# A gated delta-rule transformer block on one core: the keys' squared norms from one wide squaring and a sum along the rows, together with a later read of a scratch block, one more step in the key stage, an earlier half of the output squares, and other buffer counts

## Chip, cores, metric

The kernel runs on one core of a Trainium2 chip. The metric is device time in microseconds (us) of one execution. The kernel before took 2166.83 us, the median of 3 runs (2163.37 to 2167.89).

## What is computed

The reference is one adaptive-layernorm block over x of shape 8 x 256 x 256 (batch, tokens, channels). A small matrix product of a conditioning vector gives shifts, scales and gates. The first half is a gated delta-rule attention with 16 key heads of width 128 and 32 value heads (two for each key head):

```python
qkv_c = sum((xp[:, j:j + Tq, :] * conv_w[:, j] for j in range(KC)))      # causal convolution, 4 taps
q = _l2norm(qkv_c[..., :QD].reshape(Bq, Tq, NK, DK))
k = _l2norm(qkv_c[..., QD:2 * QD].reshape(Bq, Tq, NK, DK))
def step(S, inp):
    q_t, k_t, v_t, b_t, d_t = inp
    Sk = jnp.einsum('bhi,bhipj->bhpj', k_t, S)
    dv = b_t[..., None] * (v_t - Sk)
    S = S * d_t[:, :, None, :, None] + jnp.einsum('bhi,bhpj->bhipj', k_t, dv)
    return (S, jnp.einsum('bhi,bhipj->bhpj', q_t, S))
out = out * rms * norm_w                       # rms over each value head
y = (out * silu(z)) @ W_out.T
```

The second half is a gated feed-forward of inner width 1024 in which the two largest magnitudes of every four are kept. All arithmetic is in float32.

## The kernel before

**Tiling.** Two batch rows (512 tokens) are treated together as one pair; there are 4 pairs. Four key heads are one group, so there are 16 groups. The recurrence is rewritten in chunks of 128 tokens: for every chunk a triangular matrix built from k k^T and the decays is inverted, first in 32 x 32 blocks and then, by levels, up to 128 x 128.

**Stages of a head.** `stage_a` (L479) prepares a key head of the next group: projection `ps_k` (L432), convolution to `k_t` (ScalarE L418, three VectorE steps L420), squared norms (`norms2`, L441), the row `bk` (L507), the diagonal `diag` on GpSimd (L516), a scan `e` on VectorE (L551), the matrix `a_t` (L563), and four DMAs of its diagonal blocks to the scratch `scr` in DRAM (L572). Its `yield`s are the points at which other work is put in between. `stage_b` (L577) runs once a group: it loads the scratch of all four heads as `blk` (L584), makes the negated transpose `xb` of it on ScalarE (L586), solves the 32 x 32 blocks by 30 pairs of VectorE instructions (L592, L598), and stores two results (L602, L604). `levels` (L662) reads them back (L675, L678, L681) and merges the blocks on TensorE, beginning with `ps_w` (L691). `prepare` (L607) makes queries, values and gates of a head (`cv`, `gz`). `attend` (L752), once for each of the pair's two rows, makes the outputs `o`, their mean squares `ss` (L845), a reciprocal root on GpSimd, and `og` (L861). `shares` (L883) multiplies by the output weights. `feed_forward` (L160) and `fill` (L262) take tokens through a pool `feed_pool`; the last four feed-forward units run in the pool `tail`.

**The squared norms.** `norms2` transposes a 128 x 512 tile by TensorE into one PSUM bank and then, for each of its four 128 x 128 parts, runs a ScalarE squaring with an accumulator output (L451). It is called for the keys (`n2k`) by `stage_a` and for the queries (`n2q`) by `prepare`. The bank is one of three that `ps_in` has; the projections `ps_qv`, `ps_k`, the gates `ps_z` and the shares `ps_y` use the same three.

**What sets the order.** The loop over heads keeps a list of generators and takes one step of each in turn; after each turn it calls `along()` (L1073), which advances the background of the next group (`ahead`, L967: all `stage_a` steps at cost 3.0 each, all `stage_b` steps at cost 1.0 each) until its done cost reaches a share of `work` (L997), so that the background is due after three quarters of the group's 32 nominal turns. A scheduler then takes this order as priorities, assigns buffers, and lays down one fixed order of instructions for each engine. An instruction that waits holds up all that stands behind it on its engine or DMA queue.

The lines around `work` and its use:

```python
work = 3.0 * 4 * GH + Q
while done < work * rounds / (total * 3 / 4):
    step = next(background, None)
```

Of the kernel before, what the change touches and what calls it, by code (L numbers as in the profile page):

```python
# [11 lines left out]
F32 = mybir.dt.float32  # L12
AF = mybir.ActivationFunctionType
ALU = mybir.AluOpType
AX = mybir.AxisListType
# [3 lines left out]
P = 128  # L19
# [5 lines left out]
Q = 32  # L25
NQ = P // Q
GH = 4
# [21 lines left out]
def adaln_block(  # L49
# [18 lines left out]
    nc = tc.nc  # L68
    NT, C = x.shape
# [3 lines left out]
    NCH = T // P  # L73
# [9 lines left out]
    small = ctx.enter_context(tc.tile_pool(name="small", bufs=4))  # L83
# [76 lines left out]
    def feed_forward(pool, b, n, y_all, w_bufs=3):  # L160
# [3 lines left out]
        gate = pool.tile([P, C], F32, tag="gate", name="gate")  # L164
        nc.sync.dma_start(out=gate, in_=gate_dram[b, 0].partition_broadcast(P))
        yield
        yg = pool.tile([P, 1, C], F32, tag="tokens", name="yg")
        nc.vector.tensor_tensor(out=yg[:, 0, :], in0=y_all[:, b % 2 * NCH + n, :], in1=gate, op=ALU.mult)
        nc.vector.tensor_tensor(out=x1, in0=x1, in1=yg, op=ALU.add)
        gate = pool.tile([P, C], F32, tag="gate", name="gate")  # L170
        nc.sync.dma_start(out=gate, in_=gate_dram[b, 1].partition_broadcast(P))
        xn = pool.tile([P, 1, C], F32, tag="tokens", name="xn")
        normed(xn, x1)
        yield
        h2 = pool.tile([P, CC, P], F32, tag="h2", name="h2")
# [4 lines left out]
        for j in range(NG):  # L180
            hj = hid[:, j]
            for i in range(0, 4, 2):
                ps = bank(ps_inv, [P, 2, 2, P], "ps_ff")
                for a in range(2):
# [14 lines left out]
                    out=hj[:, i : i + 2], in0=hj[:, i : i + 2], in1=ps[:, 1], op=ALU.mult  # L199
# [10 lines left out]
            for lag, cmp in ((1, c1), (2, c2), (3, c3)):  # L210
                nc.vector.tensor_tensor(
                    out=cmp, in0=mag[:, : 4 - lag], in1=mag[:, lag:], op=ALU.is_ge
# [12 lines left out]
                out=d[:, 2:4], in0=d[:, 2:4], scalar=1.0, in1=c2, op0=ALU.add, op1=ALU.subtract  # L225
            )
            yield
            for i, m, least in ((0, 3, 1.5), (3, 1, -0.5)):
                nc.vector.scalar_tensor_tensor(
                    out=hj[:, i : i + m],  # L230
# [7 lines left out]
        ps = bank(ps_inv, [P, C], "ps_out")  # L238
        for j in range(NG):
            for i in range(0, 4, 2):  # L240
                w = pool.tile([P, 2, C], F32, tag="w_ff", name="w_dn", bufs=w_bufs)
                nc.sync.dma_start(out=w, in_=w_down[j, i // 2])
                for l in range(2):
# [4 lines left out]
                        start=(j + i + l == 0),  # L248
                        stop=(j == NG - 1 and i + l == 3),
                    )  # L250
        res = pool.tile([P, C], F32, tag="tokens", name="res")
        nc.vector.tensor_tensor(out=res, in0=gate, in1=ps, op=ALU.mult)
        nc.vector.tensor_tensor(out=res, in0=res, in1=x1[:, 0, :], op=ALU.add)
        nc.sync.dma_start(out=out_v[:, NCH * b + n, :], in_=res)
# [7 lines left out]
    def fill(pool, bp, h_bp, xs):  # L262
# [4 lines left out]
        for i in range(2):  # L267
            b = 2 * bp + i
            for n0 in range(0, NCH, NCH if xs else 1):
                n1 = NCH if xs else n0 + 1  # L270
                if xs:
                    x1, xn = xs[0][:, NCH * i : NCH * (i + 1)], xs[1][:, NCH * i : NCH * (i + 1)]
                else:
                    x1 = pool.tile([P, 1, C], F32, tag="x1", name="x0")
                    xn = pool.tile([P, 1, C], F32, tag="tokens", name="xn0")
                nc.sync.dma_start(out=x1, in_=x_v[:, NCH * b + n0 : NCH * b + n1, :])
                normed(xn, x1)
                yield
                done = modulated(xn, b, h_bp[:, :, i * T + n0 * P : i * T + n1 * P], 0)
                if bp == 0:  # L280
                    begun["tokens"] = done
                yield
        NT4 = 2 * NCH
        ps = bank(ps_mix, [P, NT4, 2, NV], "ps_ba")
        for n in range(NT4):
# [14 lines left out]
            out=a_pre,  # L300
            in0=ps[:, :, 1, :],
            in1=bias_bc[:, None, :].to_broadcast([P, NT4, NV]),
            op=ALU.add,
# [10 lines left out]
            out=y, in0=w, scalar=-1.0, in1=y, op0=ALU.add, op1=ALU.subtract  # L314
# [22 lines left out]
        ps = bank(ps_mix, [NV, NT4, P], "ps_dt")  # L337
# [14 lines left out]
        ps = bank(ps_mix, [P, 2, 2, NV], "ps_g")  # L352
# [13 lines left out]
    with ExitStack() as scope:  # L366
# [4 lines left out]
        mixp = scope.enter_context(tc.tile_pool(name="mixp", bufs=4))  # L371
# [69 lines left out]
        def norms2(src, name):  # L441

            n2 = small.tile([P, 2, NCH], F32, tag=name, name=name)
            ps = bank(ps_in if name == "n2k" else ps_in, [P, 2, NCH, P], f"ps_{name}")
            for i in range(2):
                for n in range(NCH):
                    nc.tensor.transpose(ps[:, i, n, :], src[:, i, n * P : (n + 1) * P], ident)
            for i in range(2):
                for n in range(NCH):
                    junk = mixp.tile([P, P], F32, tag="junk", name="junk", bufs=2)  # L450
                    nc.scalar.activation(  # L451
                        junk, ps[:, i, n, :], AF.Square, accum_out=n2[:, i, n : n + 1]
                    )
            return n2
# [24 lines left out]
        def stage_a(kh, bp, hp, wk, h_bp, scr):  # L479
# [16 lines left out]
            else:  # L496
# [11 lines left out]
                out=bk,  # L508
# [13 lines left out]
            with tc.issue_after(done.ins):  # L522
                nc.gpsimd.tensor_tensor(out=nk, in0=n2f, in1=halves[:, : 2 * NCH], op=ALU.pow)
            yield rec

            e = rec_pool.tile([P, 2, NS, PE1], F32, tag="e", name="e")
            rec["e"] = e
# [46 lines left out]
                )  # L574
            yield rec

        def stage_b(scr, scr_x, scr_y):  # L577

            blk = single.tile([P, Q, Q], F32, tag="blk", name="blk")
            nc.sync.dma_start(out=blk, in_=scr)  # L584
            xb = single.tile([P, Q, Q], F32, tag="xb", name="xb")
            nc.scalar.activation(xb, blk.rearrange("p a b -> p b a"), AF.Copy, scale=-1.0)  # L586
            nc.gpsimd.memset(xb.rearrange("p a b -> p (a b)")[:, :: Q + 1], 1.0)
            yield
            for j in range(1, Q - 1):
                m = Q - 1 - j  # L590
                tmp = single.tile([P, m, j], F32, tag="tmp", name="tmp", bufs=2)
                nc.vector.tensor_tensor(  # L592
                    out=tmp,
                    in0=blk[:, j, j + 1 :, None].to_broadcast([P, m, j]),
                    in1=xb[:, j, None, 0:j].to_broadcast([P, m, j]),
                    op=ALU.mult,
                )
                solved = nc.vector.tensor_tensor(  # L598
                    out=xb[:, j + 1 :, 0:j], in0=xb[:, j + 1 :, 0:j], in1=tmp, op=ALU.subtract
                )  # L600
                yield solved.ins
            nc.sync.dma_start(out=scr_x, in_=xb)  # L602
            nc.scalar.copy(blk, xb.rearrange("p a b -> p b a"))
            nc.sync.dma_start(out=scr_y, in_=blk)  # L604
            yield
# [146 lines left out]
        def attend(rec, i, cv, gz, eps_q, tt, og_t):  # L752
# [71 lines left out]
            for h in range(2):  # L824
                nc.tensor.matmul(ps_o[:, h, :], lhsT=aq[:, 0, h, :], rhs=u0[:, h, :], start=True, stop=True)  # L825
            nc.scalar.copy(o[:, 0], ps_o)
            yield

            ps_u = bank(ps_mix, [P, 2, P], "ps_u1")
# [8 lines left out]
            nc.vector.tensor_tensor(out=o[:, 1], in0=o[:, 1], in1=ps_o, op=ALU.add)  # L838


            ss = small.tile([P, NCH, 2], F32, tag="ss", name="ss")
            for n in range(NCH):
                for h in range(2):
                    junk = mixp.tile([P, P], F32, tag="junk", name="junk", bufs=2)
                    nc.scalar.activation(  # L845
                        junk, o[:, n, h, :], AF.Square, accum_out=ss[:, n, h : h + 1]
                    )
            nc.vector.scalar_tensor_tensor(  # L848
                out=ss,
                in0=ss,  # L850
# [143 lines left out]
            yield from fill(feed_pool, bp, h_t, None)  # L994
            nc.sync.dma_start(out=h_dram[bp], in_=h_t)

        work = 3.0 * 4 * GH + Q  # L997
        recs, scratch = [], []
        xs = [rec_pool.tile([P, 2 * NCH, C], F32, tag="a_t", name=f"xs{i}", bufs=5) for i in range(2)]
        sel = selectors()  # L1000
# [204 lines left out]
```

## Time and profile before

| what | value |
|---|---|
| median of 3 runs | 2166.83 us |
| the profiled execution's own time | 2163.81 us |
| its span in the profile | 2162.0 us |
| granted TensorE clock | 0.987 of full speed |
| chain that ended last, by engine | PE 64%, ACT 12%, DVE 11%, DMA 7%, issue 4% |
| DMA queue q1 | 163.34 MB, 28.2% of 16 engines' span |
| DMA issue blk<-scr, 16 times 512 KB | 3.6 us from issue to landing |
| DMA issue scr<-a_t, 256 times 32 KB | 2.6 us from issue to landing |

PE is TensorE's matmul, PEld its weight load, DVE VectorE, ACT ScalarE, POOL GpSimd, SP the engine that issues most DMAs. In a row of groups the columns are: line, engine, operation, output<-inputs with shapes and count; then busy us in all and mean ns of one; then the engine's idle time just before these instructions and what ended it. In a row of waits: the engine and line that waited, what it waited for, us in total, times, the longest in us. In a row of windows: the stretch in us, its length, busy us of each engine (with the number of instructions), granted clock, DMA share and GB/s. Ends of matmuls are modelled, and a float32 matmul shows as two records.

### The profile page before, as it was taken

The numbers are of one execution on the slowest core, as the hardware profiler recorded it, in microseconds if no ns is written. First come the engines' busy times: TensorE is split into PE (matmuls) and PEld (weight loads), VectorE is DVE, ScalarE is ACT, GpSimd is POOL, SyncE is SP. The second block draws the span as 40 slices with busy tenths as digits, with TensorE's granted clock in tenths as the row PEclk, the third lists the DMA queues.
The fourth block names the chain that finished last, engine by engine and source line by source line (L and its number), as shares of the span: only waits on it lengthen the run. The fifth ranks groups of instructions, "written<-read, shape, count | busy, mean of one in ns | idle before, by whom it ended". The sixth has DMA issues, their size and how long they took to land.

```text
span 2162.0 us, 46431 instructions
## 1 busy us (share of the span) xinstructions
PE 2061.9 (95%) x16684; PEld 1634.1 (76%) x16684; DVE 1663.1 (77%) x4039; ACT 1373.6 (64%) x4552; POOL 370.7 (17%) x375
## 2 busy tenths in 40 slices
PE   8889999999999999999999999999999989999998
PEld 5567777777777777778777787787878777787887
DVE  6688686877869578797878868788797868879457
ACT  3577676866656566666566656666676666666652
POOL 3120212112120111212121121211202012121010
PEclk9999999999999999999999999999999999999999
DMA  4242423333342443434434343443434344343336
GB/s 137 85 117 65 105 68 101 91 83 91 101 117 67 124 115 95 132 90 109 119 90 118 104 109 94 122 117 87 132 92 108 92 115 120 108 113 90 75 91 212
DMA packets 324517, 226.85 MB, mean 105 GB/s; under 512 B 254520, under 2 KB 266168, under 8 KB 324288
## 3 DMA queue, kind: packets, MB, share of 16 engines
q1 hardware_dynamic: 304416, 163.34, 28.2%
q10 hardware_dynamic: 19872, 60.54, 8.8%
q8 instruction: 133, 2.18, 0.4%
q14 instruction: 96, 0.79, 0.1%
HBM read 186.28 MB, written 29.12 MB: 100 GB/s over the span
## 4 chain that ended last, share of the span: by engine, by line
PE 64%; ACT 12%; DVE 11%; DMA 7%; issue 4%; SPq 1%; POOL 1%; ACTq 0%; DVEq 0%; POOLq 0%
PE ps_y L891 9%; PE ps_qv L432 8%; PE ps_z L634 8%; PE ps_ks L806 5%; PE ps_ff L190 3%; PE ps_k L432 3%; PE ps_o L825 2%; PE ps_u L831 2%; DVE cv L420 2%; PE ps_out L244 2%; DMA blk<-scr 2%; PE ps_kk L532 2%; DMA scr<-a_t 2%; PE ps_u L798 2%; DVE a_t L563 2%
## 5 line engine op out<-in xcount | busy, mean ns | idle before, releaser
L420 DVE SCALAR_TENSOR_TENSOR cv<-ps_qv,conv_sb,cv 128x510 f32<-128x510 f32 (+1 forms) x564 | 410.2, 737 | 43.5 <-ACT cv L418 39.4
L432 PE MATMUL ps_qv<-h_bp,wh 128*128 128x512 f32 x768 | 365.1, 601 | 12.0 <-ACT junk L451 8.4
L105 POOL TENSOR_TENSOR rs<-ss,minus_halves 128x4 f32<-128x4 f32 x128 | 135.2, 1058 | 1019.6 <-DVE ss L848 1018.6
L634 PE MATMUL ps_z<-wh,h_bp 128*128 128x256 f32 x1024 | 250.4, 390 | 9.5 <-ACT junk L451 6.6
L891 PE MATMUL ps_y<-wo,og_p 128*128 128x256 f32 x1024 | 236.8, 380 | 0.8 <-ACT og_p L878 0.8
L432 PEld LDWEIGHTS ps_qv<-h_bp,wh 128*128 128x128 f32 x768 | 133.3, 191 | 118.9 <-issue 99.3
L634 PEld LDWEIGHTS ps_z<-wh,h_bp 128*128 128x128 f32 x1024 | 189.1, 193 | 38.5 <-ACT junk L451 9.9
L891 PEld LDWEIGHTS ps_y<-wo,og_p 128*128 128x128 f32 x1024 | 187.4, 190 | 22.8 <-ACT og_p L878 1.1
L418 ACT ACTIVATE cv<-ps_qv,conv_sb 128x512 f32<-128x512 f32 x188 | 129.6, 690 | 117.6 <-PE ps_qv L432 117.0
L592 DVE TENSOR_TENSOR tmp<-blk,xb 128x30 f32<-128x30 f32 (+14 forms) x480 | 156.8, 327 | 57.8 <-ACT xb L586 48.7
L516 POOL TENSOR_TENSOR diag<-consts,bk 128x1032 f32<-128x1032 f32 x64 | 122.8, 1919 | 384.5 <-DVE bk L507 352.6
L845 ACT ACTIVATE junk<-o 128x128 f32<-128x128 f32 x512 | 153.3, 303 | 41.4 <-DVE o L838 35.0
L551 DVE TENSOR_TENSOR_SCAN e<-dbc,diag 128x1032 f32<-128x1032 f32 x60 | 137.9, 2298 | 39.3 <-POOL diag L516 36.3
L598 DVE TENSOR_TENSOR xb<-xb,tmp 128x30 f32<-128x30 f32 (+14 forms) x480 | 157.0, 327 | 9.5
L420 DVE SCALAR_TENSOR_TENSOR k_t<-ps_k,conv_sb,k_t 128x510 f32<-128x510 f32 (+1 forms) x189 | 139.7, 740 | 24.8 <-ACT k_t L418 22.9
L861 DVE SCALAR_TENSOR_TENSOR og<-o,rs,gz 128x128 f32<-128x128 f32 x512 | 145.9, 344 | 10.3 <-POOL rs L105 8.1
L772 ACT ACTIVATE vn<-ps_v,nk 128x256 f32<-128x256 f32 x256 | 106.2, 483 | 61.4 <-PE ps_v L767 61.2
L806 PE MATMUL ps_ks<-u,cross 128*128 128x128 f32 x1024 | 141.0, 280 | 0.9 <-ACT u L800 0.9
L806 PEld LDWEIGHTS ps_ks<-u,cross 128*128 128x128 f32 x1024 | 130.8, 194 | 9.5 <-issue 3.3
L190 PE MATMUL ps_ff<-h,w_ff 128*128 128x128 f32 x1024 | 130.0, 277 | 3.2 <-ACT h L149 2.2
L190 PEld LDWEIGHTS ps_ff<-h,w_ff 128*128 128x128 f32 x1024 | 122.5, 192 | 7.8 <-ACT h L149 3.2
L432 PE MATMUL ps_k<-h_bp,wk 128*128 128x512 f32 x256 | 124.9, 613 | 1.6 <-ACT junk L451 1.2
(177 smaller groups left out, 4274.8 us busy)
## 6 DMA issues: line engine op xcount, KB each, us to landing
wh<-in_w_heads ACTq DMA_DIRECT2D x64, 640.0 KB, 4.0
w_ff<-in_w_ff SPq DMA_DIRECT2D x128, 256.0 KB, 2.9
dbc<-d_dram SPq DMA_DIRECT2D x60, 516.0 KB, 4.3
wo<-in_w_heads ACTq DMA_DIRECT2D x32, 512.0 KB, 3.7
w_dn<-in_w_down SPq DMA_DIRECT2D x64, 256.0 KB, 3.8
wk<-in_w_keys SPq DMA_DIRECT2D x16, 512.0 KB, 4.5
scr<-a_t SPq DMA_DIRECT2D x256, 32.0 KB, 2.6
blk<-scr SPq DMA_DIRECT2D x16, 512.0 KB, 3.6
```

What stands on the lines that cost most here:

```text
L105: nc.gpsimd.tensor_tensor(out=out, in0=in_, in1=minus_halves[:, :n], op=ALU.pow)
L190: nc.tensor.matmul(ps[:, a, l, :], lhsT=w[:, k, l, :], rhs=h2[:, k, :], start=(k == 0), stop=(k == CC - 1),)
L420: nc.vector.scalar_tensor_tensor(out=dst[:, :, d:], in0=ps[:, :, : T - d], scalar=taps[:, KC - 1 - d : KC - d], in1=dst[:, :, d:], op0=ALU ...
L432: nc.tensor.matmul(ps.rearrange("p b t -> p (b t)"), lhsT=w[k], rhs=h_bp[:, k, :], start=(k == 0), stop=(k == CC - 1),)
L551: nc.vector.tensor_tensor_scan(e.rearrange("p i s t -> p (i s t)"), dbc.rearrange("p i f -> p (i f)"), diag.rearrange("p s t -> p (s t)"), ...
L592: nc.vector.tensor_tensor(out=tmp, in0=blk[:, j, j + 1 :, None].to_broadcast([P, m, j]), in1=xb[:, j, None, 0:j].to_broadcast([P, m, j]), ...
L598: solved = nc.vector.tensor_tensor(out=xb[:, j + 1 :, 0:j], in0=xb[:, j + 1 :, 0:j], in1=tmp, op=ALU.subtract)
L634: nc.tensor.matmul(ps[:, n, :], lhsT=h_bp[:, k, i * T + n * P : i * T + (n + 1) * P], rhs=wh[:, k * 640 + 384 : (k + 1) * 640], start=(k = ...
L806: nc.tensor.matmul(ps_ks[:, ct, h, :], lhsT=cross[:, h, ct, :], rhs=u0[:, h, :], start=True, stop=True)
L845: nc.scalar.activation(junk, o[:, n, h, :], AF.Square, accum_out=ss[:, n, h : h + 1])
L861: nc.vector.scalar_tensor_tensor(out=og[:, n, h, :], in0=o[:, n, h, :], scalar=rs[:, 2 * n + h : 2 * n + h + 1], in1=gz[:, i, n, h, :], op ...
L891: nc.tensor.matmul(ps_y[:, n, :], lhsT=og_p[:, j // 2, i, n, j % 2, :], rhs=wo[:, j // 2, j % 2, :], start=(j == 0), stop=(j == 3),)
```

## The change

Five edits:

1. **Key norms.** In `norms2`, for `n2k` alone, one ScalarE squaring of all 512 columns writes a tile `sq` (one buffer), and one VectorE `tensor_reduce` sums each of the four 128-column parts into `n2`. The queries keep the four squarings with accumulators.
2. **A later read of `blk`.** `stage_b` yields seven times (`LANDS`) between the issue of the load of `blk` and the ScalarE instruction that reads it; `work` grows from 80 to 99 to count these and the steps of edit 3.
3. **One more yield** in `stage_a` after the norms, except in the first group.
4. **Output squares.** In `attend` the two squarings of the first chunk's output are placed right after the copy that makes it, two yields earlier; those of the second chunk stay.
5. **Buffers.** The tag `tokens` has 2 buffers everywhere: before it had 1 in `feed_pool` and 4 in `tail`.

```diff
-        yg = pool.tile([P, 1, C], F32, tag="tokens", name="yg")
+        yg = pool.tile([P, 1, C], F32, tag="tokens", name="yg", bufs=2)
...
+            if name == "n2k":
+                sq = mixp.tile([P, 2, NCH, P], F32, tag="sq", name="sq", bufs=1)
+                nc.scalar.activation(sq, ps, AF.Square)
+                nc.vector.tensor_reduce(out=n2, in_=sq, axis=AX.X, op=ALU.add)
+                return n2
...
             yield rec
+            if not first:
+                yield rec
...
+        LANDS = 7
...
             nc.sync.dma_start(out=blk, in_=scr)
+            for _ in range(LANDS):
+                yield None
             xb = single.tile([P, Q, Q], F32, tag="xb", name="xb")
...
             nc.scalar.copy(o[:, 0], ps_o)
+            ss = small.tile([P, NCH, 2], F32, tag="ss", name="ss")
+
+            def squares(n):
+                for h in range(2):
+                    junk = mixp.tile([P, P], F32, tag="junk", name="junk", bufs=2)
+                    nc.scalar.activation(
+                        junk, o[:, n, h, :], AF.Square, accum_out=ss[:, n, h : h + 1]
+                    )
+
+            squares(0)
             yield
...
+            squares(1)
...
-        work = 3.0 * 4 * GH + Q
+        work = 3.0 * 5 * GH + Q + LANDS
```

The same `bufs=2` is given to `xn`, `xn0` and `res`.

More of the change, by code (lines that the diff above doesn't have):

```diff
@@ L171, in feed_forward @@
         nc.sync.dma_start(out=gate, in_=gate_dram[b, 1].partition_broadcast(P))
-        xn = pool.tile([P, 1, C], F32, tag="tokens", name="xn")
+        xn = pool.tile([P, 1, C], F32, tag="tokens", name="xn", bufs=2)
         normed(xn, x1)
@@ L250, in feed_forward @@
                     )
-        res = pool.tile([P, C], F32, tag="tokens", name="res")
+        res = pool.tile([P, C], F32, tag="tokens", name="res", bufs=2)
         nc.vector.tensor_tensor(out=res, in0=gate, in1=ps, op=ALU.mult)
@@ L274, in fill @@
                     x1 = pool.tile([P, 1, C], F32, tag="x1", name="x0")
-                    xn = pool.tile([P, 1, C], F32, tag="tokens", name="xn0")
+                    xn = pool.tile([P, 1, C], F32, tag="tokens", name="xn0", bufs=2)
                 nc.sync.dma_start(out=x1, in_=x_v[:, NCH * b + n0 : NCH * b + n1, :])
@@ L838, in attend @@
             nc.vector.tensor_tensor(out=o[:, 1], in0=o[:, 1], in1=ps_o, op=ALU.add)
[L841 to L847, printed above, removed]
+            squares(1)
             nc.vector.scalar_tensor_tensor(
```

## Prediction

> **What bounds the kernel now.** I read the busy shares first, then the waits, then the windows, then a timeline of one window.
>
> ```profile
> PE 2061.9 (95%) x16684; PEld 1634.1 (76%) x16684; DVE 1663.1 (77%) x4039; ACT 1373.6 (64%) x4552; POOL 370.7 (17%) x375
> ```
>
> TensorE is the bound: 2061.9 of 2162.0 us, so 100.1 us of idle is nearly all that an edit without matmuls can win, and this change adds and removes none. The question is where TensorE idles. I cut the span at 100 and 2080 us (start and tail), and laid one window over each of the 15 later places where ScalarE makes `xb` (L586), from 5 us before to 10 us behind it:
>
> ```profile
> 100.00:2080.00 1980.00, 1906.39 (x15797) 1516.60 (x15794) 1545.27 (x3704) 1300.58 (x4332) 343.17 (x340) 0.99 0.37 101
> ...
> 641.00:656.00 15.00, 12.25 (x118) 9.94 (x118) 10.19 (x29) 10.32 (x30) 1.63 (x3) 0.89 0.26 86
> ...
> 909.00:924.00 15.00, 12.92 (x127) 10.09 (x127) 10.26 (x33) 10.40 (x33) 2.41 (x4) 1.00 0.21 74
> ...
> 1161.00:1176.00 15.00, 11.33 (x119) 9.16 (x120) 10.24 (x30) 10.25 (x30) 1.63 (x3) 1.00 0.22 77
> 1301.00:1316.00 15.00, 11.07 (x124) 8.57 (x122) 10.61 (x30) 10.57 (x35) 1.28 (x2) 1.00 0.31 85
> ...
> sum 226.00, PE 191.86 PEld 152.00 DVE 168.42 ACT 166.64 POOL 26.26; mean PE 12.79 PEld 10.13 DVE 11.23 ACT 11.11 POOL 1.75
> ```
>
> Between 100 and 2080 TensorE idles 1980.0 - 1906.4 = 73.6 us. The 15 windows, 11% of that stretch, hold 226.0 - 191.9 = 34.1 of it. Elsewhere the rate is 39.5 / 1754 = 2.3%, so the windows hold 34.1 - 5.2 = 28.9 us in excess. The waits and the timeline (ScalarE, then TensorE) say why:
>
> ```profile
> DVE tmp L592 <- ACT xb L586: 48.7, 15, 5.9
> ACT xb L586 <- DMA blk<-scr: 45.3, 14, 5.1
> PE ps_kq L779 <- ACT vn L772: 16.0, 11, 3.0
> PE ps_qv L432 <- ACT junk L451: 8.4, 10, 1.2
> DVE e L551 <- POOL diag L516: 36.3, 23, 2.1
> DVE yg L168 <- DMA out<-res: 11.3, 6, 3.5
> ```
>
> ```profile
> 1165.90 1.96 ACT L586 ACTIVATE xb<-blk 128x1024 f32<-128x1024 f32 x1 [4.37 <-DMA blk<-scr]
> ...
> 1168.62 0.82 ACT L772 ACTIVATE vn<-ps_v,nk 128x256 f32<-128x256 f32 x2
> 1169.33 0.28 ACT L451 ACTIVATE junk<-ps_n2q 128x128 f32<-128x128 f32 x1
> ...
> 1169.58 0.29 ACT L451 ACTIVATE junk<-ps_n2q 128x128 f32<-128x128 f32 x1
> ```
>
> ```profile
> 1169.49 0.70 PE L779 MATMUL ps_kq<-cv,k_t 128*128 128x256 f32 x2 [2.69 <-ACT vn L772]
> ```
>
> ScalarE stands 4.37 us before `xb` until `blk` lands. Work that is ready (`vn`, output squares, `w`) is queued behind, and TensorE then waits 2.69 us for `vn`. VectorE cannot start the solve either.
>
> **The change, part by part.**
>
> *Later read of `blk`.* No instruction is added; the order moves. I counted, in the built order of both programs, the ScalarE work between the last `og_p` ahead of `xb` and `xb`, at the page's durations. In the seven groups whose windows begin at 641, 781, 909, 1036, 1301, 1428 and 1556 it grows by 2.2 to 4.8 us (at 909, two `cv` and four squares become `mag`, four squares, one `cv`, four `vn` and two `w`). ScalarE waited 3.1 to 4.6 us there. TensorE's idle in these seven is 2.75 + 3.46 + 2.08 + 2.55 + 3.93 + 1.29 + 1.56 = 17.6 us, 15.2 in excess of 2.3%. I take three quarters: -11 us. At 1161 and 1677 the built order has 0.9 us less ahead of `xb`, at 1815 and 1937 under 1 us more, and in groups 1 to 4 somewhat less: nothing there. Bounds: 0 (landing is late as well) and -28.9. At the start the order now has a `cv` copy (0.57) and four `taps` (1.28) ahead of `xb`; `raw`, for which TensorE waits 5 us, comes some 1.6 us sooner: -1.6.
>
> *Key norms.* ScalarE removes 256 squarings and their reads of the accumulator. They start 0.25 us apart (1169.33, 1169.58), so four cost 1.0 us plus a 0.2 us tail. The single squaring is not in the trace; the nearest row is the 128x512 copy of `raw` out of PSUM, 0.58 us. ScalarE saves about 0.45 x 64 = 29 us, at 64% busy worth nothing by itself. The bank is free some 0.5 us sooner: TensorE's waits for L451 are 8.4 (`ps_qv`) + 6.6 (`ps_z`) + 1.2 (`ps_k`) = 16.2 us for keys and queries, which have as many squarings each; half of the keys' 8.1 goes: -4 (bounds 0 and -8).
>
> VectorE gets 64 sums of 512 columns. The operation isn't in the trace either; near it:
>
> ```profile
> L788 DVE TENSOR_TENSOR aq<-ps_kq,e 128x512 f32<-128x512 f32 x128 | 85.9, 677 | 10.0 <-ACT cross L786 9.4
> ```
>
> That gives 64 x 0.68 = 43 us. Here a rule speaks against the change: the Trainium skill (VectorE: DVE Perf Modes, Rules for kernel authors) calls `tensor_reduce` the slowest VectorE operation, never above its basic rate, to be avoided on a hot path. At the basic rate of that page's add formula, (512 + 151) / 0.96 = 691 ns, an estimate, the sum is 44 us, the same as by the row; both say that more VectorE time is added than ScalarE time is saved, on the busier engine. What decides is where. Windows over the 15 solves, from the first `tmp` to the last `xb`, add up to:
>
> ```profile
> sum 697.00, PE 668.74 PEld 539.60 DVE 647.33 ACT 444.49 POOL 60.82; mean PE 44.58 PEld 35.97 DVE 43.16 ACT 29.63 POOL 4.05
> ```
>
> VectorE is 93% busy there. The sums lie in `stage_a`, outside: there it is busy 1545.3 - 647.3 = 898 of 1283 us, 70%, with 385 us idle to take 43. As a bound below, half of 0.68 if one input is read at double rate; above, 1 us: 22 to 64 us. I take 43 and charge TensorE with a tenth: +4 (bounds 0 and +15). If the cover were gone, all 43 would show. In the key chain the sum takes the place of the three squarings saved: 0.68 against 0.6, nothing. Behind a sum that waits for its squaring stand convolution steps that free `ps_in` banks.
>
> *One more yield, and `work`.* Order only. The built order has less work between `bk` and the scan, so VectorE stands longer before `e` (the 36.3 us row): worked out from `diag` at 1.9 us, about 6.5 instead of 3.7 us in a typical group. In the same 385 us of idle; within the +4.
>
> *Earlier output squares.* 256 of 512 squarings move, none is added. In the steady part ScalarE is not late for them; at the last head two squares (0.6 us) leave the path: -0.5.
>
> *Buffers.* The 11.3 us that VectorE waits for `out<-res` go; TensorE rarely waits for that engine: -1 (0 to -3). In the tail, 4 to 2 buffers could hold up `xn`; but its four units already follow each other at 3.2 us (the `ps_h` at 2107.98, 2111.24, 2114.41, 2117.39), and the built order there is unchanged: 0, at most +2. SP's DMAs keep count and size; `blk` is no later in its queue by more than one weight load.
>
> Sum: -11 - 1.6 - 4 + 4 - 0.5 - 1 = -14.1. Span 2162.0 - 14.1 = 2147.9; plus 1.8 around it (2163.81 - 2162.0) 2149.7; the median of the runs stands 3.0 above the profiled execution: 2153.
>
> **The rivals.**
>
> *All the windows clear.* If `vn` and `w` no longer stand behind a wait in any group, the 28.9 us go instead of 11: -32, 2135. For it: the same wait in 12 of 15 windows. Against: in two groups the order moves nothing ahead of `xb`, and in groups 1 to 4 ScalarE is full.
>
> *TensorE comes too early to the blocks (slower).* In the built order the TensorE work between a group's last `ps_kk` and the next group's first `ps_w`, by start-to-start times, shrinks from 72.8 to 66.6 us in four groups and by 2 to 5 in three more (in three others it grows by 3.4). VectorE's work from the last `a_t` to the end of the solve shrinks only by 0.4 to 3.0. If the solve does not start sooner, since scr and `blk` land as before and VectorE's added sums delay `a_t`, TensorE waits at `ps_w` by the difference, in all 24 us, and the -11 fails: 24 + 4 - 1.6 - 4 - 1.5 = +21, 2188. It decides once `x_even` lands after TensorE's arrival. For it: `ps_w` now follows the issue of `x_even` by 2 to 4 us, hardly more than a landing. Against: the wait for `blk`, 3 to 4 us, lies in that chain, and the waits at `ps_w` for `x_even` are 1.9 us in all now. Half of it would be 2177.
>
> *Nothing moves.* The stalls shift to other places in a new order; TensorE's idle stays near 100 us: 2163 to 2171.
>
> **How the numbers follow.** Forecast (2140 to 2162) 0.47; windows clear or better 0.15; no change 0.13; slower 0.25, most of it below 2182. A difference of 0.2%, 4.3 us, is what a measurement can tell from none. Faster 0.62, same 0.13, slower 0.25. The range 2128 to 2182 leaves out some 6% below and 10% above.
>
> **What would show it.** Right: idle of ScalarE before `xb` under 25 us in all, `ps_kq` for `vn` under 8, windows around `xb` idle under 23; `tensor_reduce` near 0.68 us; DVE near 1700 us busy. Wrong: idle at `ps_w` for `x_even` or at `ps_t` up by over 10 us, new TensorE waits for VectorE's `cv`, or TensorE idle near 100 us as before.

## The result, and the profile after

| what | before | after |
|---|---|---|
| median of the runs beside each other | 2162.97 us (22 runs) | 2167.14 us (22 runs) |
| ratio, after to before | | 1.0025, interval 1.0015 to 1.0036 |
| the same again, on another chip (e13, below) | 2170.27 us (27 runs) | 2175.13 us (12 runs): 1.0027, 1.0008 to 1.0047 |
| span of the profiled execution | 2162.0 us | 2166.2 us |
| granted clock in it | 0.987 | 0.983 |

One run of the 22 took 3437 us at a clock of 0.56; it is left out of the ratio. The kernel became slower by a quarter of a per cent where 14 us of gain had been worked out. The busy row of the page after, and the long middle stretch with the windows around `xb` (now L598; the same 15 places, 5 us before to 10 us behind it):

```profile
PE 2072.0 (96%) x16684; PEld 1637.6 (76%) x16684; DVE 1698.0 (78%) x4103; ACT 1348.3 (62%) x4103; POOL 363.5 (17%) x375
```

```profile
100.00:2080.00 1980.00, 1911.00 (x15809) 1515.59 (x15805) 1576.97 (x3761) 1279.12 (x3925) 336.03 (x339) 0.99 0.37 101
...
sum 225.00, PE 197.98 PEld 150.75 DVE 178.75 ACT 173.68 POOL 24.49; mean PE 13.20 PEld 10.05 DVE 11.92 ACT 11.58 POOL 1.63
```

TensorE's idle time fell, from 100.1 to 2166.2 - 2072.0 = 94.2 us, and in the windows from 34.1 to 225.0 - 198.0 = 27.0 us. Yet its busy time grew by 10.1 us with the same 16684 matmuls. In some stretches the granted clock is 0.50, and there a record of `ps_qv` takes 1061 instead of 592 ns (medians). Such stretches add up to 75.1 us of the span after and 55.3 us before; TensorE is busy in 66.1 and in 51.1 us of them. Half of the difference, 7.5 us, is an estimate of what they add to the busy time. So most of this run's loss is not in any row of waits. A typical run loses less: the clock of the fast runs is 0.9848 on the mean, and 0.983 in the profiled one. The waits after:

```profile
DVE e L558 <- POOL diag L521: 50.6, 30, 2.1
DVE tmp L604 <- ACT xb L598: 33.6, 14, 4.3
ACT xb L598 <- DMA blk<-scr: 28.3, 15, 4.5
DVE yg L168 <- DMA gate<-gate_dram: 16.0, 9, 4.6
PE ps_u L810 <- ACT u L812: 15.2, 8, 3.0
PE ps_w L743 <- ACT x_top L732: 8.8, 4, 5.9
PE ps_kq L791 <- ACT vn L784: 3.4, 4, 1.4
```

ScalarE's wait before `xb` fell from 45.3 to 28.3 us and TensorE's wait for `vn` from 16.0 to 3.4, as meant. Two rows are new: TensorE waits 15.2 us for `u`, and VectorE waits 16.0 us for the row of the gate, where it had waited 11.3 us for a store (`out<-res`). The timeline of one group shows where the first comes from, first ScalarE, then TensorE:

```profile
917.28 1.98 ACT L598 ACTIVATE xb<-blk 128x1024 f32<-128x1024 f32 x1 [1.71 <-DMA blk<-scr]
...
919.55 0.68 ACT L418 ACTIVATE cv<-ps_qv,conv_sb 128x512 f32<-128x512 f32 x1
...
920.38 0.84 ACT L798 ACTIVATE cross<-ps_kq,e 128x256 f32<-128x256 f32 x2
...
922.05 0.42 ACT L812 COPY u<-ps_u 128x256 f32<-128x256 f32 x1
```

```profile
922.52 0.71 PE L810 MATMUL ps_u<-vn,t_inv 128*128 128x128 f32 x4 [2.67 <-ACT u L812]
```

`vn` and `w` are now ahead of `xb`. What stands behind it instead is the next link of the same chain: `cross`, then `u`. TensorE had waited for `vn`; it now stands 2.67 us for `u`.

### The profile page after: what moved, and what is told of

Same layout as the page of the kernel before. It is cut to its first block, busy times and chain, and to the rows that moved or that the text cites. A ratio compares the mean times of both kernels' runs of the same rounds, so it can differ in the third digit from the quotient of the medians.

```text
span 2166.2 us, 45917 instructions
## 1 busy us (share of the span) xinstructions
PE 2072.0 (96%) x16684; PEld 1637.6 (76%) x16684; DVE 1698.0 (78%) x4103; ACT 1348.3 (62%) x4103; POOL 363.5 (17%) x375
## 5 line engine op out<-in xcount | busy, mean ns | idle before, releaser
L420 DVE SCALAR_TENSOR_TENSOR cv<-ps_qv,conv_sb,cv 128x510 f32<-128x510 f32 (+2 forms) x564 | 408.4, 735 | 40.6 <-ACT cv L418 38.2
L432 PE MATMUL ps_qv<-h_bp,wh 128*128 128x512 f32 x768 | 372.6, 607 | 7.9 <-DVE cv L420 5.9
L646 PE MATMUL ps_z<-wh,h_bp 128*128 128x256 f32 x1024 | 245.5, 383 | 3.9 <-ACT junk L456 3.3
L907 PE MATMUL ps_y<-wo,og_p 128*128 128x256 f32 x1024 | 241.8, 383 | 0.0
L190 PE MATMUL ps_ff<-h,w_ff 128*128 128x128 f32 x1024 | 134.7, 281 | 2.6 <-ACT h L149 1.7
L653 ACT ACTIVATE gz<-ps_z 128x512 f32<-128x512 f32 x128 | 76.0, 597 | 80.8 <-PE ps_z L646 80.2
```

The lines of the kernel that those rows point to most:

```text
L190: nc.tensor.matmul(ps[:, a, l, :], lhsT=w[:, k, l, :], rhs=h2[:, k, :], start=(k == 0), stop=(k == CC - 1),)
L420: nc.vector.scalar_tensor_tensor(out=dst[:, :, d:], in0=ps[:, :, : T - d], scalar=taps[:, KC - 1 - d : KC - d], in1=dst[:, :, d:], op0=ALU ...
L432: nc.tensor.matmul(ps.rearrange("p b t -> p (b t)"), lhsT=w[k], rhs=h_bp[:, k, :], start=(k == 0), stop=(k == CC - 1),)
L646: nc.tensor.matmul(ps[:, n, :], lhsT=h_bp[:, k, i * T + n * P : i * T + (n + 1) * P], rhs=wh[:, k * 640 + 384 : (k + 1) * 640], start=(k = ...
L907: nc.tensor.matmul(ps_y[:, n, :], lhsT=og_p[:, j // 2, i, n, j % 2, :], rhs=wo[:, j // 2, j % 2, :], start=(j == 0), stop=(j == 3),)
```

## Experiments

Two explanations stood against each other at first: that the later read and the steps around it moved stalls instead of removing them, and that the sums on VectorE are the cost. The letters in the expectations are each batch's own, explained there. Each kernel was measured beside the kernel before on the same chip; a ratio is always to that.

**One edit at a time.** e1 has the key norms alone:

```diff
+            if name == "n2k":
+                sq = mixp.tile([P, 2, NCH, P], F32, tag="sq", name="sq", bufs=1)
+                nc.scalar.activation(sq, ps, AF.Square)
+                nc.vector.tensor_reduce(out=n2, in_=sq, axis=AX.X, op=ALU.add)
+                return n2
```

> The kernel before with the key norms' edit alone (one ScalarE squaring of 512 columns, one VectorE sum). Theory A (the waits move: what the later read of blk wins at vn comes back at u behind the 2 us instruction that makes xb, at the gate load, and as half-clock stretches of TensorE; the norms themselves cost little): ratio 0.998 to 1.002. Theory B (the added VectorE sums, 64 of 0.69 us, are what made the change slower): 1.003 to 1.008, with VectorE's busy time up by some 38 us and TensorE waiting more for VectorE.

Measured: 0.998 (0.9968 to 0.9991), 2162.97 against 2168.17 us. The second explanation fell: the sums with the single squaring are, alone, a gain of some 4 us. ScalarE's wait before `xb` fell to 29.6 us here too, with no later read: a new order of the instructions is enough for that. e2 has the four other edits without it:

> The changed kernel with the old key norms (edits 2 to 5 alone). Theory A: about as slow as the changed kernel, 1.001 to 1.004, with TensorE waiting some 15 us for u. Theory B: faster than before, 0.992 to 0.998, since the sums are gone.

Measured: 1.0022 (1.0011 to 1.0034). The other edits together are the loss, though not by the wait that was expected: TensorE waits 3.2 us for `u`, not some 15. e3 is the later read alone:

```diff
+            for _ in range(7):
+                yield None
...
-        work = 3.0 * 4 * GH + Q
+        work = 3.0 * 4 * GH + Q + 7
```

> The kernel before with the later read of blk alone (seven yields and 7 more in work). Theory A: ScalarE's wait for blk falls from 45 us to under 30, TensorE's wait for vn falls, its wait for u rises to over 8 us, ratio 0.997 to 1.003. The prediction's step (-11 us for this edit, nothing behind it): 0.993 to 0.996 and no new wait for u.

Measured: 1.0173 (1.0147 to 1.0198). The wait for `vn` is still there:

```profile
PE ps_kq L781 <- ACT vn L774: 18.2, 7, 4.4
PE ps_u L833 <- ACT o L822: 7.8, 10, 1.4
PE ps_qv L432 <- ACT junk L451: 7.8, 10, 1.1
```

The edit for which the prediction gave -11 us costs 38 us when it is made alone. The mean time from the last `a_t` of a group to its `xb` grew from 8.1 to 10.2 us, and the chain from there to TensorE's first `ps_w` of the group, that time included, from 62.8 to 65.8 us. e4 has the buffers alone (`bufs=2` at the four token tiles), e5 the yield alone (with `work` 92), e6 the yield and the later read (with `work` 99), e8 the earlier squares alone:

> The kernel before with two buffers for the tag tokens alone. The prediction's step: VectorE's wait of yg for out<-res (11 us) is gone, -1 us, 0.998 to 1.001. Theory A: the wait is replaced by one of yg for the load of gate, of about the same size, ratio 0.998 to 1.003.

> The kernel before with the one more yield in stage_a alone (work 92 instead of 80). Theory A (each edit gives the scheduler another order, and stalls of TensorE move from place to place with it): within 0.5% of before on either side, with other waits at the head of TensorE's list. Theory C (the yield is what carries the later read of blk: alone the later read cost 1.7%, so the two must act together): 0.996 to 1.000.

> The kernel before with the later read of blk and the one more yield (edits 2 and 3, work 99). Theory A: 1.000 to 1.006; the wait at vn is smaller, others are new. Theory C: 0.994 to 0.999, so the 1.7% of the later read alone is gone and a gain is left.

> The kernel before with the earlier squares of the first chunk alone (edit 4). The prediction's step: -0.5 us, 0.999 to 1.001. Theory A: two squares now stand ahead of the scaling of the second chunk's output on ScalarE and the order is new: 0.997 to 1.005, with the sign open.

Measured: e4 1.0024 (1.0012 to 1.0036), with VectorE's wait for the gate as in the changed kernel (14.0 us); e5 1.0039 (1.0023 to 1.0054); e6 1.0089 (1.0067 to 1.0111), slower than either of its expectations; e8 1.0002 (0.9987 to 1.0017). The single edits multiply to 0.998 x 1.0173 x 1.0039 x 1.0002 x 1.0024 = 1.022, and the whole is 1.0025. They don't add up: yield and later read together (1.0089) cost less than the later read alone.

**Is the length of `xb` the new stall?** e7 is the changed kernel with `xb` made in two halves of 1 us, a step of other work between them:

```diff
-            nc.scalar.activation(xb, blk.rearrange("p a b -> p b a"), AF.Copy, scale=-1.0)
+            turned_blk = blk.rearrange("p a b -> p b a")
+            nc.scalar.activation(xb[:, : Q // 2], turned_blk[:, : Q // 2], AF.Copy, scale=-1.0)
+            yield None
+            nc.scalar.activation(xb[:, Q // 2 :], turned_blk[:, Q // 2 :], AF.Copy, scale=-1.0)
```

> The changed kernel with the ScalarE instruction that makes xb cut into two of 16 rows, the second one turn later (six yields ahead instead of seven). Theory A: the 2 us of xb ahead of u are what the new wait of 15 us at ps_u is made of, so that wait falls under 8 us and the time goes to 0.998 to 1.001 of before. Rival (the wait at u comes from the rest of ScalarE's queue, squares and cross): the wait stays over 12 us, 1.001 to 1.005.

Measured: 1.003 (1.0014 to 1.0045); TensorE's wait for `u` 12.7 us against 15.2. Taking the suspected 2 us apart gains nothing: that the stall stands behind `xb` is where it went, and the length of `xb` is not what it costs.

**What does another order do, and what do more sums do?** e9 is the kernel before with `work` 81 for 80; e18 is the changed kernel with 100 for 99. Nothing else is touched in either.

> The kernel before with the planner's total raised by 1 (work = 81 instead of 80). No instruction is added, removed or made longer or shorter; only the order in which the groups' steps are laid between each other is dealt out anew. Theory A (each edit acts mostly by the order that it deals, and not by its own cost): the time moves by more than 0.2% though nothing else changed, as likely as not slower, 2171 to 2186 us (raising the total by 12 made it 0.4% slower). Rival (the orders are all alike, and a few tenths of a per cent come from each edit's own instructions): within 0.15% of the kernel before, 2164 to 2170 us, with TensorE's waits for ScalarE's vn near 16 us and ScalarE's wait before xb near 45 us as there.

> The changed kernel with the planner's total at 100 instead of 99: every instruction and buffer as in the changed kernel, another order. If the single-buffered loads are the cost: they stay (VectorE's wait for gate and x near 28 us), and the time is the changed kernel's, 1.001 to 1.004 of the kernel before. If it is one order's bad luck: it moves by more than 0.2% from 1.0027, to below 1.0005 or above 1.005.

Measured: e9 0.9992 (0.9979 to 1.0005); e18 1.0136 (1.0117 to 1.0154), in which TensorE's wait for `x_top` is 18.4 us against 8.8 and that of `ps_z` for the single squarings 13.0 against 3.3. One unit in a planner's total is worth nothing that can be measured in one program and 1.1% (1.0136 over 1.0027, about 24 us) in the other. In both, thousands of instructions changed places. So an order alone can cost more than any single edit's own arithmetic here, and the ratio of a kernel in which the order changed is not by itself the price of its edit.

e10 makes each key sum twice, the first into a tile that nobody reads; e11 treats the queries like the keys (`if name in ("n2k", "n2q")`).

> The kernel before with the key norms alone by one squaring and one sum, and each sum made twice, the first time into a spare tile that nobody reads: 64 more sums of 512 columns, and the order of all else is the same as with the norms alone. It adds 64 x 0.69 = 44 us to VectorE (1695 to about 1739 us busy). If the sums lie under cover: within 0.1% of the norms alone (0.997 to 0.999 of the kernel before). The prediction's charge, a tenth of it on TensorE: +4 us, 1.000. If the cover were gone: +44 us, 1.018. In the start the first sums lie on the path (keys' norms before the first scale), so up to +3 us there in any case.

> The kernel before with the norms of the queries as well as the keys by one squaring and one sum (both share one tile for the squares). ScalarE saves another 29 us, VectorE takes another 44 us (about 1735 to 1740 busy). If what helped with the keys was the bank that one squaring frees sooner: TensorE's remaining waits for the single squarings (ps_qv, ps_z) fall by another 5 us or so, and the time is 0.996 of the kernel before. Rival (the gain with the keys came from the order, and the queries' sums fall where VectorE is busiest, in the solve): no better than the norms alone, 0.999 to 1.004, with VectorE's tmp or TensorE's ps_w waiting longer.

Measured: e10 1.0061 (1.0047 to 1.0075); e11 1.0285 (1.0264 to 1.0305). In e10 the scheduler dealt another order, which I had not expected, so its 0.8% over e1 is no clean price of 43 us of sums: TensorE's stalls stand elsewhere (`ps_z` for `gz` 22.8 us, new; `ps_kq` for `vn` 2.0 instead of 15.6). e11 contradicts the hope plainly, and its row says why:

```profile
PE ps_n2q L447 <- ACT gz L646: 18.4, 7, 4.0
PE ps_w L696 <- DMA x_even<-scr_x: 10.3, 9, 2.3
PE ps_kq L784 <- DVE o L843: 10.2, 6, 3.6
```

Of the queries' 64 sums 31 lie in a solve, where VectorE is nearly full, against 10 of the keys' 64: a solve takes 52.8 us on the mean, against 46.0 in e1, and TensorE then waits at `ps_w` for `x_even`. So the place of a sum counts more than its 0.68 us. How much of the loss is that, and how much the new order and the clock (0.967 in this trace, 0.986 in e1's), is not taken apart.

**Which edit makes the whole slow?** e12 is the changed kernel with its old token buffers (one in the feed, four in the tail).

```diff
-        yg = pool.tile([P, 1, C], F32, tag="tokens", name="yg", bufs=2)
+        yg = pool.tile([P, 1, C], F32, tag="tokens", name="yg")
```

and likewise for `xn`, `xn0` and `res`.

> The changed kernel with its token tiles in four buffers as before (all its other edits kept). If the fewer buffers cost what they cost alone (0.24%), by the wait of the gated sum for its gate row instead of for a store: VectorE's wait of yg for the gate falls below 10 us from 16, TensorE's wait of ps_w for x_top from 8.8 to 5 or less, and the time is 1.000 of the kernel before, 2166 to 2168 us against 2171 to 2173 for the changed kernel on this chip. Rival (the fewer buffers cost nothing by themselves, and what they showed alone was the clock granted to that order): 1.002 to 1.004, like the changed kernel.

Measured: 0.9977 (0.9966 to 0.9989), 2158.02 against 2163.14 us. Without the buffer edit the change is a gain of 5 us; with it, on two chips, a loss of 5 to 6. So about 10 us hang on the edit that was charged with -1. Its order is almost the changed kernel's (on TensorE 329 of 16684 places hold another instruction), so the two profiles can be laid over each other matmul by matmul. The changed kernel falls behind at few places: by some 2.5 us near 25, by 3.9 near 250, by 2.4 near 731, by 4 near 2000 and near 2100 us; it wins some 7 us back elsewhere. At 250, VectorE of the changed kernel:

```profile
251.65 0.43 DVE L131 BATCH_NORM_STATS2 stats<-x 128x6 f32<-128x256 f32 x1 [2.10 <-DMA x<-in_x]
...
252.21 0.65 DVE L451 TENSOR_REDUCE n2k<-sq 128x4 f32<-128x512 f32 x1
...
253.60 2.10 DVE L137 TENSOR_SCALAR xn<-x,mv,rstd 128x256 f32<-128x256 f32 x1
255.62 1.52 DVE L420 SCALAR_TENSOR_TENSOR cv<-ps_qv,conv_sb,cv 128x510 f32<-128x510 f32 x2
257.05 0.68 DVE L800 TENSOR_TENSOR aq<-ps_kq,e 128x512 f32<-128x512 f32 x1
```

and VectorE of e12 at the same work:

```profile
249.62 0.68 DVE L451 TENSOR_REDUCE n2k<-sq 128x4 f32<-128x512 f32 x1
...
251.78 0.43 DVE L131 BATCH_NORM_STATS2 stats<-x 128x6 f32<-128x256 f32 x1 [0.86 <-DMA x<-in_x]
...
252.34 0.72 DVE L420 SCALAR_TENSOR_TENSOR cv<-ps_qv,conv_sb,cv 128x510 f32<-128x510 f32 x1
253.09 0.75 DVE L420 SCALAR_TENSOR_TENSOR cv<-ps_qv,conv_sb,cv 128x508 f32<-128x508 f32 x1
253.75 0.68 DVE L800 TENSOR_TENSOR aq<-ps_kq,e 128x512 f32<-128x512 f32 x1
```

With a second token buffer the scheduler lays the next rows' statistics ahead of the key sum, and their `xn` ahead of `cv` and `aq`. There VectorE waits 2.10 us for `x`, whose tile has one buffer still, and `xn` takes 2.10 us instead of 0.41. `cv` and `aq` are 3.3 us later, but by 2.1 us the kernel was behind already. TensorE waits, and the stretches around it (here 3.4 us each; the columns behind the five engines are granted clock, DMA share and GB/s) show a second bill:

```profile
257.79 0.71 PE L810 MATMUL ps_u<-vn,t_inv 128*128 128x128 f32 x4 [0.89 <-DVE aq L800]
261.28 2.07 PE L432 MATMUL ps_qv<-h_bp,wh 128*128 128x512 f32 x2 [2.78 <-DVE cv L420]
```

```profile
252.70:256.10 3.40, 3.40 (x28) 2.26 (x28) 3.22 (x7) 2.05 (x5) 3.03 (x3) 1.00 0.51 195
256.10:259.50 3.40, 1.51 (x12) 1.13 (x10) 3.36 (x4) 0.19 (x1) 0.46 (x1) 1.00 0.13 39
259.50:262.90 3.40, 1.62 (x2) 0.83 (x3) 3.40 (x8) 1.88 (x6) 0.00 (x0) 0.50 0.52 156
262.90:266.30 3.40, 3.40 (x20) 1.53 (x19) 1.83 (x5) 0.81 (x2) 0.55 (x1) 0.50 0.09 24
266.30:269.70 3.40, 3.40 (x34) 3.28 (x36) 3.40 (x7) 0.37 (x2) 0.00 (x0) 1.00 0.25 39
```

After the stretch in which TensorE worked 1.51 of 3.40 us, the clock is 0.50 in the next, and once more after that one (1.62). e12 waits here as well, 2.39 us against 0.89 + 2.78, and keeps its clock:

```profile
257.65 1.98 PE L432 MATMUL ps_qv<-h_bp,wh 128*128 128x512 f32 x4 [2.39 <-DVE cv L420]
251.00:269.00 18.00, 15.61 (x132) 12.50 (x131) 16.57 (x32) 10.18 (x28) 3.41 (x3) 1.00 0.29 82
```

The other place, near 731: VectorE of the changed kernel, then TensorE.

```profile
731.40 0.42 DVE L168 TENSOR_TENSOR yg<-y,gate 128x256 f32<-128x256 f32 x1 [4.55 <-DMA gate<-gate_dram]
731.74 2.30 DVE L558 TENSOR_TENSOR_SCAN e<-dbc,diag 128x1032 f32<-128x1032 f32 x1
733.96 0.41 DVE L725 STREAM_TRANSPOSE low<-ps_t 32x256 f32<-32x256 f32 x1
```

```profile
735.16 0.47 PE L743 MATMUL ps_w<-x_top,a_t 64*64 64x64 f32 x2 [5.94 <-ACT x_top L732]
```

And e12:

```profile
722.77 2.31 DVE L558 TENSOR_TENSOR_SCAN e<-dbc,diag 128x1032 f32<-128x1032 f32 x1 [1.81 <-POOL diag L521]
726.43 0.42 DVE L168 TENSOR_TENSOR yg<-y,gate 128x256 f32<-128x256 f32 x1 [1.36 <-DMA out<-res]
726.77 0.43 DVE L725 STREAM_TRANSPOSE low<-ps_t 32x256 f32<-32x256 f32 x1
```

```profile
728.00 0.47 PE L743 MATMUL ps_w<-x_top,a_t 64*64 64x64 f32 x2 [4.67 <-DMA dbc<-d_dram]
```

In e12 the scan `e` ran before `yg`; in the changed kernel it stands between `yg` and `low`. But TensorE stood here in e12 too, 4.67 us against 5.94. And in e13, a second trace of the changed kernel, where `yg` waits 3.21 us for the gate and the scan stands as here, the kernel loses nothing to e12 at this place. So neither wait accounts for much of the 10 us. The sums say where they are (the changed kernel in e13, then e12, then the kernel before with the buffers alone, e4):

```profile
PE 2072.2 (95%) x16684; PEld 1635.6 (75%) x16684; DVE 1698.9 (78%) x4103; ACT 1349.5 (62%) x4103; POOL 363.6 (17%) x375
PE 2059.7 (96%) x16684; PEld 1629.1 (76%) x16684; DVE 1695.4 (79%) x4103; ACT 1352.4 (63%) x4103; POOL 362.8 (17%) x375
PE 2071.1 (95%) x16684; PEld 1639.0 (75%) x16684; DVE 1664.4 (77%) x4039; ACT 1368.9 (63%) x4548; POOL 368.8 (17%) x375
```

TensorE idles 94.2 us in the changed kernel's first trace and 2172.7 - 2072.2 = 100.5 in its second, 96.5 in e12, 100.1 in e4 as in the kernel before. So the buffer edit adds no idle time on which the two traces of the changed kernel agree; it adds busy time, 12 us (9 in e4). Stretches at half clock add up to 75.1 and 69.2 us against 45.8 in e12, and to 73.3 in e4 against 55.3 in the kernel before. At or just behind each of the five places above, the changed kernel's first trace has such stretches, 34 us in all; e12 has 3.4 us there.

The gate's tile has one buffer. The unit before reads it in its last product `res`, so the next gate cannot be loaded before that, and then takes 3.2 us from issue to landing (median of 32). Before, `yg` had to wait for the store of `res` anyway, which hid this; the added buffer only unmasked it. It did not make it longer: in e12 the gate's row at 726.43 had landed 0.51 us, the store 0.12 us before `yg` began. Every kernel here that has the new token buffers and one gate buffer shows eight or nine such waits (12.3 to 18.8 us in all) and none for the store; every kernel with the old ones shows three to nine for the store (5.4 to 17.9 us) and none for the gate.

Three kernels test whether the loads into single buffers carry the loss. e15 gives back only the tail's four buffers, with the order on every engine unchanged. e14 adds a second gate buffer (and takes one from the squares' scrap tile `junk`). e17 adds second buffers for gate and `x1`. In e17 the tile of `h2` holds the comparison `c2`; against what its expectation says, `h2` is still read by the second half of the inner width, so its result is not that of the reference; the instructions and sizes are the same.

```diff
-        gate = pool.tile([P, C], F32, tag="gate", name="gate")
+        gate = pool.tile([P, C], F32, tag="gate", name="gate", bufs=2 if w_bufs == 3 else 4)
```

> The changed kernel itself, beside the next three on one chip. 1.0025 of the kernel before (1.0015 to 1.0036) as first measured; the others are read against it.

> The changed kernel with four token buffers in the tail as before, and two in the feed; the order of instructions is that of the changed kernel on every engine. If the tail's fewer buffers cost: the time from 2080 us to the end falls by 2 to 4 us (it was 3.7 longer than before), 1.0005 to 1.0015 of the kernel before. If they do not: the time of the changed kernel, within 0.1% of it, and the 10 us lie in the feed.

> The changed kernel with two buffers for the gate row in the feed (and one instead of two for the squares' scrap tile, to make room). Theory G (with two token buffers the gated sum no longer waits for the store of the unit before it, and so is laid earlier and waits instead for a gate row whose only buffer is read by that unit's last product): VectorE's wait of yg for the gate falls from 16.0 to under 5 us, TensorE's wait of ps_w for x_top from 8.8 to under 5, and the time to 0.996 to 0.999 of the kernel before. Rival (the wait for the gate is harmless, and the difference of the buffer edit is that of the order it deals, with its granted clock): the gate wait goes as well, but the time stays at 1.001 to 1.005.

> The changed kernel with two buffers in the feed for x1 and gate as for the token tiles (room made by letting the second comparison use the tile of h2, which is dead by then, and the third a token tile). Theory L (VectorE stands before loads into single-buffered tiles): its waits for x<-in_x (stats, x) and for the gate fall from about 28 us together to under 15 us, and the time to 0.996 to 1.000 of the kernel before. Rival (order): those waits fall as well, but the time stays above 1.002, with TensorE's stalls elsewhere (ps_u, ps_w, ps_qv).

Measured: e13 1.0027 (1.0008 to 1.0047); e15 1.0046 (1.0028 to 1.0065), so the tail holds none of it; e17 1.0 (0.9987 to 1.0012), with no wait for the gate left, 13.3 us for `x` in the statistics, and TensorE's wait for `x_top` down to 3.1 us; e14 1.017 (1.0142 to 1.0199), where the wait for the gate went and this row came:

```profile
DVE x L169 <- DMA x<-in_x: 20.6, 9, 5.1
```

In e14 the wait moved to the next tile with one buffer, and the time went up by 1.4%, which the wait's 5 us more cannot explain; another order was dealt too, and `junk` with one buffer took part (TensorE's wait of `ps_qv` for it: 10.0 us against 1.2). e17 fits the theory of the single-buffered loads, e14's wait does, its time does not. With e18 in mind, two orders that agree with a theory are not proof of it.

Last, e16 is e12 without the later read (`work` 92):

> The changed kernel with its old token buffers and without the later read of blk (LANDS gone, the planner's total 92): the key norms, the one more yield, and the earlier squares. If the later read gains in this combination what the prediction gave it (-11 us): 0.5% slower than with it, 1.002 to 1.004 of the kernel before, with ScalarE's wait before xb near 45 us instead of 34. If it gains nothing, as the wait merely moves: 0.996 to 0.999, like the version with it.

Measured: 0.9998 (0.9985 to 1.0012), against 0.9977 (0.9966 to 0.9989) for e12 on another chip. So in this company the step from e16 to e12 is about -0.2%, some 4 us, and not the -11 of the sum; the order changed with it, so even that is no clean price. ScalarE's wait before `xb` is 21.0 us in e16, less than in e12 with the later read (34.2): that row had not been a measure of what the read costs.

Two versions beat the kernel before, and with it the changed one: the key norms alone (e1, 0.998) and the change without its buffer edit (e12, 0.9977).

## Why the prediction was wrong

*Buffers, -1: the step that failed.* It booked the 11.3 us wait for a store as gone, and put what the edit does to the order, and TensorE's clock, at nothing. The wait was not gone: the gate's row lands some 0.4 us before the store did, so `yg` waited for that (16.0 us in all). And "TensorE rarely waits for that engine" was read under the old order. Size: 10 us the other way (0.9977 to 1.0025 or 1.0027), so 11 of the 19 us between the sum of -14 and the measured +5; the buffers alone cost 5 us (e4). That the loss comes and goes with the buffer edit is shown by e12, e13 and e4. What carries it is not shown. In the traces it stands in TensorE's busy time, with more stretches at half clock, and not in a larger sum of idle; near 731 us, where the gate's wait is longest, e13 has that wait and loses nothing. e2, which has the buffer edit too, is slow without more of such stretches. Why this order meets more such stretches stays open, and that another order with the same buffers would not is a rival that e18 leaves standing.

*Later read, -11: mis-sized.* TensorE's idle in the windows fell by 7.1 us, the wait for `vn` by 12.6, that for `u` rose by 13.9 (1.3 to 15.2). The prediction asked what stands behind `xb` now and not what would stand there next. Alone the edit comes with a loss of 1.7% (e3), among the others with a gain of about 0.2% (e16 to e12), both with another order. A three-quarter share of counted idle had no ground in the trace.

*Start, -1.6.* The first `ps_w` is at 95 us instead of 93; in e12 it is at 93. The loss there goes with the buffers in these single traces.

*Key norms: -4 + 4, and 0.68 us a sum.* The sum's duration was right:

```profile
L451 DVE TENSOR_REDUCE n2k<-sq 128x4 f32<-128x512 f32 x64 | 43.3, 676 | 23.9 <-ACT sq L450 23.4
```

The squaring was 0.607 for 0.58 us. Alone they give 0.2%, about 4 us (1.9 to 6.9), where the two terms cancelled. TensorE's waits for squarings fell from 16.2 to 5.9 us in e1, by more than the bound of 8, so the freed bank may well be the larger term; how much of that is the new order is not shown. That sums are dear where VectorE is full, as e11 suggests, is what the prediction said of the solve.

*Earlier squares, -0.5.* 1.0002: as predicted, nothing that can be seen.

*The clock had no term.* Stretches at half clock grew by 19.8 us, an estimated 7.5 us of the profiled run. An idle time that is short in the sum of waits can cost as much again. It is not the whole of the busy time either: e2 is busy 2071.8 us with only 47.8 us at half clock, and why is open. The Trainium skill (TensorE: Matmul & The Clock Gate, Why this matters for your kernels) warns of idle gaps above about 3 us; by that rule none of the changed kernel's TensorE waits shown here but the one of 5.94 us would count. In this trace a stretch of 3.4 us with 1.89 us of idle, in pieces of 0.89 and 1.00 us within it, was followed by one at half clock. The measurement decides.

*The rivals.* "Nothing moves" (2163 to 2171) is where the time fell, and its mechanism, stalls that shift, is largely what the waits show; but it had no clock in it, so its number is in part luck. The slower rival is not what happened: `ps_w` waits 3.3 us for `x_even`, not 24.

*The signs.* Of those set for being right, the wait for `vn` (3.4 us), the sum's 0.68 us and VectorE's busy time (1698 us) came; ScalarE's wait before `xb` (28.3, not under 25) and the windows' idle (27.0, not under 23) did not. Of those set for being wrong, one came: TensorE's idle is 94.2 us, and 100.5 in e13, near the 100 of before. More busy time had no sign.

## What to carry to other kernels

A buffer that is added to one tile can move the wait to the next tile of the same chain that has only one, as it did here; follow the chain to its end before a gain is booked. Where a scheduler deals the order anew at each edit, first measure edits that change only the order: no effect smaller than their spread (here, with one such edit each, none in one program and 1.1% in another) can be put down to a mechanism. Before a wait is called the cause of a loss, look whether the faster kernel waits there too, and whether a second trace of the slower one shows it. Of a moved wait ask what stands behind it afterwards, and count idle time of TensorE by the stretches in which it lies, because the clock is charged for that as well.

## Not expected of the hardware

The granted clock and the time go together from run to run of one kernel: over the 59 runs of the kernel before on one chip, time falls by 1.4 us for each 0.001 of clock (correlation -0.74; 1.1 to 1.5 us in the four other sets of its runs). With means of 0.9848 and 0.9833 for the changed kernel and 0.9866 for e12, that relation would put some 2 to 5 of the 10 us between them down to the clock, and with 0.9824 for e4 and 0.9864 beside it all of its 5. It does not hold for every pair: e2, at 0.9885, is slower than the kernel before.

Idle time need not lie in one piece to be followed by half clock. Half-clock stretches are whole multiples of 3.41 us; in the 20 traces, cut on that grid from 25 us on, full-clock stretches in which TensorE was busy under 40% were all followed by one at half clock (124 of 124), at 40 to 60% 123 of 228, at 60 to 80% 68 of 604, above that 2 of 4343. A half-clock stretch with under 80% was always followed by another (73 of 73). Near 250, e12's wait fell across two stretches of the grid, busy 50 and 80%.

A VectorE instruction can be held by GpSimd. The `xn` of 2.10 us above began with `diag` on GpSimd and ended with it:

```profile
253.63 1.92 POOL L521 TENSOR_TENSOR diag<-consts,bk 128x1032 f32<-128x1032 f32 x1
```

In the changed kernel four VectorE instructions are longer than their group's median by over 0.3 us, 5.2 us together, and all four end within 0.15 us of a GpSimd instruction; in e11 there are 19 (22.4 us), nine of them `og`. In the kernel before there are ten (9.2 us), so none of the loss lies here. That they wait for something shared by both engines is inferred from these ends; no run here took it apart.
